# A two-layer graph network: transposes by DRAM scratch and VectorE block turns in place of TensorE, with TensorE in program order

## The chip, the core and the metric

The kernel runs on one core of a Trainium2 chip. TensorE (PE) multiplies, VectorE (DVE) and ScalarE (ACT) do elementwise work, GpSimd (POOL) one small power step, and SyncE (SP) issues the transfers. The metric is the device time of one execution in microseconds; lower is better.

## The reference

Thirty-two graphs (batches) of 512 nodes with 512 features go through two layers. All is float32.

```python
# layer 0
h = jnp.maximum(_layernorm(x, axis=-1), 0.0)
deg = jnp.sum(adj, axis=-1, keepdims=True)
agg = jnp.einsum('bij,bjf->bif', adj, h) / jnp.maximum(deg, EPS)
x = x + relu(einsum('bnf,of->bno', concatenate([h, agg], axis=2), W))
# layer 1
h = jnp.maximum(_layernorm(x, axis=-1), 0.0)
q, k = jnp.split(h @ Wqk, 2, axis=-1)
v = h @ Wv
agg = jnp.einsum('bij,bjd->bid', adj, k * mask[:, :, None])
w = inv_scale * mask * jnp.einsum('bid,bid->bi', q, agg)
x = x + softmax(w, axis=1)[:, :, None] * v
```

## The kernel before

**Algebra.** The weights are regrouped so that a batch needs six 512x512x512 products in five stages. Stage *y* is h times the second half of W (`layer0_y`, line 244). Stage *out* is h times the first half of W plus adj/deg times y (`layer0_out`, line 257; two products that accumulate together). Stage *u* is adj/deg times the masked h of layer 1 (`layer1_u`, line 299). Stage *t* is h of layer 1 times mR, where mR is Wq times Wk transposed, made once (`layer1_t`, line 310); its output is multiplied with u and summed along the rows, which gives w. Stage *v* is h of layer 1 times Wv (`layer1_v`, line 330).

**A product.** Each 512x512x512 product is cut in 2x2 blocks of 256 and computed with seven block products instead of eight (the Winograd form of Strassen's method; `product`, line 115). A tile of seven slots holds the four blocks of an operand and three sums of them; `left_sums` and `right_sums` compute the sums on DVE. Each block product is four matmuls of 128x128 by 128x256 per pair of operands (line 125). Three PSUM tiles pp, pr and pq take the results. Of these, partial results are copied to SBUF tiles called tmp by ScalarE (`keep`, line 138) before the next block product accumulates onto the same PSUM tile, so TensorE waits for such a copy if it is late. The final additions are on DVE.

**Transposes.** TensorE wants the left operand with its contraction dimension on the partitions, so h, adj/deg and h of layer 1 have to be transposed. `transpose_block` (line 160) does four 128x128 transposes on TensorE into a PSUM tile of the pool ps_t (two banks) and lets ScalarE write them to the left operand, with the ReLU on the way where it is needed. There are 12 such blocks a batch: four for h (pth, tile hT), four for adj (pta, tile aT), four for h of layer 1 (pt, tile h1T). The weights are transposed in the same way at the start (ptw).

**Order of the work.** One stream of stages runs on TensorE: for each i the loop at line 452 writes u of batch i-1, out of i, t and v of i-1, and y of i+1. After each block product, `step` (line 83) writes one piece of a list called `background`: statistics and normalization of the next batch (`prepare_h`, line 209), the degrees and transposes of adj (`prepare_a`, line 221), the normalization of layer 1 (`layer1_norm`, line 272, and `layer1_h`, line 285), and the softmax (`softmax`, line 344). What is left over is written out by `drain` at the end of a stage. This written order is a priority: a planner in the compiler orders each engine's queue by it, among the instructions that it takes to be ready, and sets the semaphores. Each engine then runs its own queue strictly in that planned order. A tile can be filled again only when the instructions that use its former content are done; how many copies a tile has ("bufs") limits how far ahead the loads run. SP issues all transfers from one queue.

The softmax needs three small matmuls on TensorE: ptop (line 363, turns the column of row maxima), pbc (line 368, spreads the maximum) and psum (line 375, sums the exponentials). Between them stand small steps on DVE and ACT. Four additions (line 380) then finish x, and one transfer stores it.

Of the kernel before, what the change touches and what calls it, by code (L numbers as in the profile page):

```python
# [21 lines left out]
def kernel(  # L22
# [26 lines left out]

    nc = tc.nc  # L50
    B, N, F = x.shape
    C = N // P
    D = F // P
    H = F // 2
    assert N == F == 512 and w0.shape[0] == F and wv.shape[1] == F
# [5 lines left out]
    ps_t = ctx.enter_context(tc.tile_pool(name="ps_t", bufs=2, space=bass.MemoryType.PSUM))  # L61
    ps_m = ctx.enter_context(tc.tile_pool(name="ps_m", bufs=5, space=bass.MemoryType.PSUM))
# [52 lines left out]
    def product(name, terms, out11, out12, out21, out22):  # L115
# [20 lines left out]
        def keep(p, what):  # L136
            t = block("tmp", 6, f"{what}_{name}")
            nc.scalar.activation(t, p, AF.Copy)  # L138
            return t
# [20 lines left out]
    def transpose_block(src, dst, func, name):  # L160

        p = ps_t.tile([P, 4, P], F32, tag="t", name=name)
        for d in range(4):
            nc.tensor.transpose(p[:, d, :], src[d], ident)  # L164
        nc.scalar.activation(dst, p.rearrange("p (a b) i -> p a b i", b=2), func)  # L165

    def row_blocks(t):
        return [t[:, ts(d, P)] for d in range(4)]

    def as_left(t, c):  # L170

        r = c // 2
        return t[:, 2 * r:2 * r + 2, :, ts(c % 2, P)]


    ident = const.tile([P, P], F32, name="ident")
    make_identity(nc, ident)
# [5 lines left out]
    X, HT, AT, DEG, Y, H1M, H1T, U, V, W = ({} for _ in range(10))  # L183

    def load_x(b):
        X[b] = big.tile([P, C, 512], F32, tag="x", bufs=3, name=f"x_{b}")
        nc.sync.dma_start(out=X[b], in_=x[b].rearrange("(c p) f -> p c f", p=P))

    def statistics(b, name):
        mv = small.tile([P, C, 2], F32, tag="mv", name=f"mv{name}")  # L190
        rstd = small.tile([P, C], F32, tag="rstd", name=f"rstd{name}")

        def one(c):
            st = small.tile([P, 6], F32, tag="st", bufs=4, name=f"st{name}_{c}")
            nc.vector.bn_stats(st, X[b][:, c, :])  # L195
            nc.vector.bn_aggr(mv[:, c, :], st)

        def last():
            nc.vector.tensor_scalar(rstd, mv[:, :, 1], LN_EPS, None, op0=ALU.add)  # L199
            nc.gpsimd.tensor_tensor(rstd, rstd, mhalf, op=ALU.pow)  # L200

        return mv, rstd, [lambda c=c: one(c) for c in range(C)] + [last]

    def normalize(o, i, mv, rstd, c):
        nc.vector.tensor_scalar(  # L205
            o, i, mv[:, c, 0:1], rstd[:, c:c + 1], op0=ALU.subtract, op1=ALU.mult
        )

    def prepare_h(b):

        mv, rstd, steps = statistics(b, f"0_{b}")
        HT[b] = slots("hT", 1, f"hT_{b}")

        def one(c):
            xn = chunk("xn", 2, f"xn_{b}_{c}")
            normalize(xn, X[b][:, c, :], mv, rstd, c)
            transpose_block(row_blocks(xn), as_left(HT[b], c), AF.Relu, f"pth_{b}_{c}")

        return steps, [lambda c=c: one(c) for c in range(C)] + left_sums(HT[b])

    def prepare_a(b):

        AT[b] = slots("aT", 2, f"aT_{b}")
        DEG[b] = small.tile([P, C], F32, tag="deg", bufs=3, name=f"deg_{b}")
        rdeg = small.tile([P, C], F32, tag="rdeg", name=f"rdeg_{b}")
        a = {}

        def one(c):
            a[c] = chunk("a", 3, f"a_{b}_{c}")
            nc.sync.dma_start(out=a[c], in_=adj[b, ts(c, P), :])  # L230
            nc.scalar.activation(a[c], a[c], AF.Copy, accum_out=DEG[b][:, c:c + 1])
            nc.vector.tensor_scalar(DEG[b][:, c:c + 1], DEG[b][:, c:c + 1], DEG_EPS, None, op0=ALU.max)
            nc.vector.reciprocal(rdeg[:, c:c + 1], DEG[b][:, c:c + 1])
            nc.scalar.activation(a[c], a[c], AF.Copy, scale=rdeg[:, c:c + 1])

        def two(c):
            transpose_block(row_blocks(a[c]), as_left(AT[b], c), AF.Copy, f"pta_{b}_{c}")

        steps = [lambda: one(0), lambda: one(1)]
        for c in range(C):  # L240
            steps.append(lambda c=c: (two(c), one(c + 2) if c + 2 < C else None))
        return steps + left_sums(AT[b])
# [14 lines left out]
    def layer0_out(b):  # L257
        def o(r, cc):
            dst = X[b][:, 2 * r:2 * r + 2, ts(cc, H)]

            def f(p, s):
                if s is not None:
                    t = block("tmp", 6, f"o_{b}_{r}{cc}")
                    add(t, p, s)
                    p = t
                nc.vector.scalar_tensor_tensor(dst, p, 0.0, dst, op0=ALU.max, op1=ALU.add)
# [5 lines left out]
    def layer1_norm(b):  # L272

        mv, rstd, steps = statistics(b, f"1_{b}")
        t = H1M[b] = slots("h1m", 1, f"h1m_{b}")

        def one(c):
            normalize(
                t[:, 2 * (c // 2):2 * (c // 2) + 2, c % 2, :],
                X[b][:, c, :].rearrange("p (a f) -> p a f", a=2), mv, rstd, c,  # L280
            )

        return steps + [lambda c=c: one(c) for c in range(C)]

    def layer1_h(b):

        t = H1M[b]
        l = H1T[b] = slots("h1T", 1, f"h1T_{b}")

        def one(c):  # L290
            k = c // 2
            src = [t[:, 2 * k + d // 2, c % 2, ts(d % 2, P)] for d in range(4)]
            transpose_block(src, as_left(l, c), AF.Relu, f"pt1_{b}_{c}")
            v = t[:, 2 * k:2 * k + 2, c % 2, :]
            nc.vector.tensor_scalar(v, v, 0.0, mraw[:, c, b:b + 1], op0=ALU.max, op1=ALU.mult)  # L295

        return [lambda c=c: one(c) for c in range(C)] + right_sums(t) + left_sums(l)

    def layer1_u(b):
        u = U[b] = big.tile([P, 4, 2, H], F32, tag="u", bufs=1, name=f"u_{b}")  # L300
# [9 lines left out]
    def layer1_t(b):  # L310
        acc = W[b] = small.tile([P, 2, C], F32, tag="acc", name=f"acc_{b}")

        def o(r, cc):
            def f(p, s):
                t = block("tmp", 6, f"t_{b}_{r}{cc}")
# [14 lines left out]
    def layer1_v(b):  # L330
        v = V[b] = big.tile([P, C, 512], F32, tag="v", bufs=1, name=f"v_{b}")
# [12 lines left out]
    def softmax(b):  # L344
# [16 lines left out]
        def s1():  # L361
            ptop = ps_s.tile([1, P], F32, tag="s", name=f"ptop_{b}")
            nc.tensor.transpose(ptop, top, ident)
# [15 lines left out]
        def s4(c):  # L379
# [4 lines left out]
            if c == C - 1:  # L384
                nc.sync.dma_start(out=out[b].rearrange("(c p) f -> p c f", p=P), in_=X.pop(b))
# [6 lines left out]
    def weight_rows(src, c, dst, name):  # L392
        t = chunk("a", 3, f"win_{name}_{c}")
        nc.sync.dma_start(out=t, in_=src[ts(c, P), :])
        transpose_block(row_blocks(t), dst, AF.Copy, f"ptw_{name}_{c}")

    def weight_right(src, dst, name):
        for c in range(4):
            weight_rows(src, c, dst[:, c // 2:4:2, :, ts(c % 2, P)], name)
# [3 lines left out]
    load_x(0)  # L403
    weight_right(w0[:, F:2 * F], w2R, "w2")
    steps, rest = prepare_h(0)
    for s in steps + rest:
        s()
    load_x(1)
# [3 lines left out]
    mask_sb = const.tile([B, N], F32, name="mask_sb")  # L412
    nc.sync.dma_start(out=mask_sb, in_=nodemask)
    wqT = big.tile([P, D, 512], F32, tag="u", bufs=1, name="wqT")
    wkT = big.tile([P, D, 512], F32, tag="v", bufs=1, name="wkT")
    for half, dst in ((0, wqT), (1, wkT)):
        for c in range(4):
            weight_rows(
                wqk[:, half * F:(half + 1) * F], c,
                dst[:, :, ts(c, P)].rearrange("p (a b) i -> p a b i", b=2), f"qk{half}",  # L420
            )
    for k in range(2):
        for dk in range(2):
            p = mm_tile(f"pm_{k}{dk}")
            d = 2 * k + dk
            for a in range(D):
                nc.tensor.matmul(
                    p.rearrange("p a f -> p (a f)"), wqT[:, a, ts(d, P)], wkT[:, a, :],
                    start=(a == 0), stop=(a == D - 1),
                )  # L430
            nc.scalar.activation(mR[:, 2 * k:2 * k + 2, dk, :], p, AF.Copy)
    for s in right_sums(mR):
        s()
    for k in range(2):
        for cc in range(2):
            nc.sync.dma_start(
                out=vR[:, 2 * k + cc, :, :],
                in_=wv[k * H:(k + 1) * H, ts(cc, H)].rearrange("(c p) f -> p c f", p=P),
            )
    for s in right_sums(vR):  # L440
        s()
    mcol = const.tile([P, C, B], F32, name="mcol")
    mraw = const.tile([P, C, B], F32, name="mraw")
    pmk = ps_t.tile([P, C, B], F32, tag="t", name="pmk")
    for c in range(C):
        nc.tensor.transpose(pmk[:, c, :], mask_sb[:, ts(c, P)], ident[:B, :B])
    nc.scalar.activation(mcol, pmk, AF.Copy, scale=scale)
    nc.scalar.activation(mraw, pmk, AF.Copy)
    drain()


    for i in range(B + 1):
        norm = prep = []
        if i > 0:
            layer1_u(i - 1)
            drain()
        if i + 1 < B:
            if i > 0:
                load_x(i + 1)
            steps, rest = prepare_h(i + 1)  # L460
            background += steps
        if i < B:
            layer0_out(i)
            drain()
            norm = layer1_norm(i)
# [44 lines left out]
```

## Time and profile before

| what | value |
|---|---|
| three runs | 2599.39, 2599.9 and 2601.4 us; median 2599.9 us |
| profiled execution | 2600.44 us, span 2598.7 us, mean granted TensorE clock 0.997 |
| TensorE busy | 2560.5 us, 99% of the span |
| VectorE, ScalarE, GpSimd busy | 1447.2, 814.0 and 65.2 us (56%, 31%, 3%) |
| HBM read, written | 72.42 MB, 33.55 MB |
| transposes on TensorE | 1,536 in the batches, 64 for the weights |

A line of a group reads: source line, engine, operation, output<-inputs, shape, count | busy time and mean duration in ns of one | idle time of the engine just before them, and what ended it. A line of a timeline reads: start, duration, engine, line, operation, output<-inputs, shape, count of merged instructions; in square brackets the idle time before it and what ended it. PE is matmuls, PEld is loading of the stationary operand. A matmul in float32 shows as two records. The busy times of successive matmuls overlap, so the spacing of their starts is the better price. A line of waits reads: who waited at which line <- for whom: total us, times, longest us. A line of a window reads: from:to, its length, then the busy time of PE, PEld, DVE, ACT and POOL, the granted clock, the mean busy share of the DMA engines and GB/s. A line of transfers reads: output<-input, issuing queue, operation, count, KB each, median us from issue to landing.

### The profile page before, as it was taken

The numbers are of one execution on the slowest core, as the hardware profiler recorded it, in microseconds if no ns is written. First come the engines' busy times: TensorE is split into PE (matmuls) and PEld (weight loads), VectorE is DVE, ScalarE is ACT, GpSimd is POOL, SyncE is SP. The second block draws the span as 40 slices with busy tenths as digits, with TensorE's granted clock in tenths as the row PEclk, the third lists the DMA queues.
The fourth block names the chain that finished last, engine by engine and source line by source line (L and its number), as shares of the span: only waits on it lengthen the run. The fifth ranks groups of instructions, "written<-read, shape, count | busy, mean of one in ns | idle before, by whom it ended". The sixth has DMA issues, their size and how long they took to land.

```text
span 2598.7 us, 31483 instructions
## 1 busy us (share of the span) xinstructions
PE 2560.5 (99%) x12548; PEld 2221.3 (85%) x12548; DVE 1447.2 (56%) x3410; ACT 814.0 (31%) x1559; POOL 65.2 (3%) x70
## 2 busy tenths in 40 slices
PE   7999999999999999999999999999999999999998
PEld 5888888888888888888888888888888888888887
DVE  4554555654655655556546556455565465565554
ACT  4333233332233332333322333323333223333222
POOL 0000000000000000000000000000000000000000
PEclk9999999999999999999999999999999999999999
DMA  4001011101111010111011110101110111101000
GB/s 159 17 17 50 33 49 49 42 24 44 38 49 49 17 49 33 49 49 46 21 45 37 49 49 17 49 33 49 49 36 30 44 38 49 49 17 49 33 21 33
DMA packets 55810, 107.98 MB, mean 42 GB/s; under 512 B 3408, under 2 KB 4432, under 8 KB 55664
## 3 DMA queue, kind: packets, MB, share of 16 engines
q1 hardware_dynamic: 55664, 105.99, 12.2%
q8 instruction: 98, 1.61, 0.3%
q14 instruction: 48, 0.39, 0.0%
HBM read 72.42 MB, written 33.55 MB: 41 GB/s over the span
## 4 chain that ended last, share of the span: by engine, by line
PE 91%; DMA 4%; ACT 2%; DVE 1%; issue 1%; POOL 0%; DVEq 0%; SPq 0%; ACTq 0%; POOLq 0%
PE pp_o L125 17%; PE pp_u L125 9%; PE pp_v L125 9%; PE pq_o L125 9%; PE pp_t L125 9%; PE pp_y L125 6%; PE pq_u L125 4%; PE pq_v L125 4%; PE pq_t L125 4%; PE pr_o L125 4%; PE pq_y L125 4%; DMA a<-in_adj_dram 3%; PE pr_v L125 2%; PE pr_t L125 2%; PE pth L164 2%; PE pt L164 2%
## 5 line engine op out<-in xcount | busy, mean ns | idle before, releaser
L195 DVE BATCH_NORM_STATS2 st<-x 128x6 f32<-128x512 f32 x256 | 165.7, 679 | 209.2 <-DMA x<-in_x_dram 207.1
L125 PE MATMUL pp_y<-w2R,hT 128*128 128x256 f32 x1024 | 253.1, 380 | 0.3 <-ACT hT L165 0.2
L125 PE MATMUL pp_u<-h1m,aT 128*128 128x256 f32 x1024 | 245.5, 382 | 0.0
L125 PE MATMUL pp_v<-vR,h1T 128*128 128x256 f32 x1024 | 242.1, 379 | 0.0
L125 PE MATMUL pp_t<-mR,h1T 128*128 128x256 f32 x1024 | 241.9, 379 | 0.0
L125 PE MATMUL pp_o<-w1R,hT 128*128 128x256 f32 x1024 | 241.9, 379 | 0.0
L125 PE MATMUL pp_o<-y,aT 128*128 128x256 f32 x1024 | 241.9, 379 | 0.0
L125 PEld LDWEIGHTS pp_o<-w1R,hT 128*128 128x128 f32 x1024 | 194.6, 190 | 26.9 <-issue 0.5
L125 PEld LDWEIGHTS pp_t<-mR,h1T 128*128 128x128 f32 x1024 | 194.6, 190 | 26.5
L125 PEld LDWEIGHTS pp_o<-y,aT 128*128 128x128 f32 x1024 | 194.6, 190 | 26.5
L125 PEld LDWEIGHTS pp_u<-h1m,aT 128*128 128x128 f32 x1024 | 189.6, 190 | 28.0 <-DVE h1m L295 0.3
L125 PEld LDWEIGHTS pp_v<-vR,h1T 128*128 128x128 f32 x1024 | 189.9, 190 | 23.3
L125 PEld LDWEIGHTS pp_y<-w2R,hT 128*128 128x128 f32 x1024 | 182.7, 191 | 19.4 <-ACT hT L165 0.5
L205 DVE TENSOR_SCALAR xn<-x,mv,rstd 128x512 f32<-128x512 f32 x128 | 67.1, 545 | 129.3 <-PE pth L164 91.4
L138 ACT ACTIVATE u_o<-pp_o 128x512 f32<-128x512 f32 x64 | 38.2, 597 | 295.2 <-PE pp_o L125 295.2
L92 DVE TENSOR_TENSOR o<-m_o,u_o 128x512 f32<-128x512 f32 x32 | 22.2, 692 | 194.1 <-ACT u_o L138 194.1
L200 POOL TENSOR_TENSOR rstd<-rstd,mhalf 128x4 f32<-128x4 f32 x64 | 64.5, 1008 | 2462.6 <-DVE rstd L199 2455.6
L125 PE MATMUL pq_u<-h1m,aT 128*128 128x256 f32 x512 | 123.6, 384 | 0.1
L125 PE MATMUL pq_y<-w2R,hT 128*128 128x256 f32 x512 | 121.7, 380 | 0.6 <-ACT m_y L138 0.4
L125 PE MATMUL pq_v<-vR,h1T 128*128 128x256 f32 x512 | 121.1, 379 | 0.0
L125 PE MATMUL pq_o<-y,aT 128*128 128x256 f32 x512 | 120.9, 379 | 0.0
L125 PE MATMUL pq_t<-mR,h1T 128*128 128x256 f32 x512 | 120.9, 379 | 0.0
(127 smaller groups left out, 4016.8 us busy)
## 6 DMA issues: line engine op xcount, KB each, us to landing
x<-in_x_dram SPq DMA_DIRECT2D x32, 1024.0 KB, 5.2
a<-in_adj_dram SPq DMA_DIRECT2D x128, 256.0 KB, 2.8
out_dram<-x SPq DMA_DIRECT2D x32, 1024.0 KB, 4.3
win_w<-in_L_gnn_W_dram SPq DMA_DIRECT2D x8, 256.0 KB, 4.7
win_qk<-in_L_gnn_Wqk_dram SPq DMA_DIRECT2D x8, 256.0 KB, 2.9
vR<-in_L_gnn_Wv_dram SPq DMA_DIRECT2D x4, 256.0 KB, 5.3
mask_sb<-in_nodemask_dram SPq DMA_DIRECT2D x1, 64.0 KB, 4.2
```

What stands on the lines that cost most here:

```text
L92: nc.vector.tensor_tensor(o, a, b, op=ALU.add)
L125: nc.tensor.matmul(p[:, rc, :], lt[:, LEFT[k], dk, ts(rc, P)], rt[:, RIGHT[k], dk, :], start=first and n == 0, stop=True, skip_group_check ...
L138: nc.scalar.activation(t, p, AF.Copy)
L164: nc.tensor.transpose(p[:, d, :], src[d], ident)
L195: nc.vector.bn_stats(st, X[b][:, c, :])
L200: nc.gpsimd.tensor_tensor(rstd, rstd, mhalf, op=ALU.pow)
L205: nc.vector.tensor_scalar(o, i, mv[:, c, 0:1], rstd[:, c:c + 1], op0=ALU.subtract, op1=ALU.mult)
```

## The change

The transposes leave TensorE. Instead:

1. The rows of a batch are laid on the partitions in another order: partition q*32+r holds, as chunk c, row q*128+c*32+r (`by_rows`). Each load or store of a batch becomes four transfers of 32 partitions.
2. The tensor to be transposed is written row by row to a scratch tensor in DRAM, chunk by chunk (`write` in `prepare_h`, `two` in `prepare_a`, `one` in `layer1_norm`).
3. `exchange` reads half of it back in four transfers, each of 32 partitions with pieces of 128 numbers (512 bytes), so that 32x32 blocks that belong on the same partitions lie there. `to_left` then turns the blocks with one VectorE instruction of 128x1024 into the left operand.
4. The normalization moves from VectorE to ScalarE (with the ReLU, `normalize`), which needs one more small VectorE step (`nmr`). In layer 1 ScalarE also scales by the mask, in place, after the unmasked rows were sent to DRAM.
5. x is loaded twice: once for the normalization (tag n), once for the residual (tag x, two buffers where there were three). u and v share one buffer, tmp has five buffers where it had six, and the matmul results have seven PSUM banks where they had five.
6. The loop is written under a manual schedule for TensorE: its instructions keep the written order, and only the other engines' are planned. The softmax steps are written ahead of the turns of layer 1's h, and the weights of layer 1 are made inside the first round of the loop (`weights_late`), after the first out.

The core of the diff:

```diff
-    ps_t = ctx.enter_context(tc.tile_pool(name="ps_t", bufs=2, space=bass.MemoryType.PSUM))
-    ps_m = ctx.enter_context(tc.tile_pool(name="ps_m", bufs=5, space=bass.MemoryType.PSUM))
+    dram = ctx.enter_context(tc.tile_pool(name="dram", bufs=2, space=bass.MemoryType.DRAM))
+    ps_m = ctx.enter_context(tc.tile_pool(name="ps_m", bufs=7, space=bass.MemoryType.PSUM))
...
-            t = block("tmp", 6, f"{what}_{name}")
+            t = block("tmp", 5, f"{what}_{name}")
...
-    def transpose_block(src, dst, func, name):
-        p = ps_t.tile([P, 4, P], F32, tag="t", name=name)
-        for d in range(4):
-            nc.tensor.transpose(p[:, d, :], src[d], ident)
-        nc.scalar.activation(dst, p.rearrange("p (a b) i -> p a b i", b=2), func)
+    def by_rows(src):
+        t = src.rearrange("(q c r) f -> q r c f", q=Q, c=C)
+        return [t[q] for q in range(Q)]
+
+    def exchange(src, name):
+        t = big.tile([P, 8, P], F32, tag="s", bufs=3, name=name)
+        for q in range(Q):
+            nc.sync.dma_start(out=t[q * R:(q + 1) * R, :, :], in_=src[:, :, ts(q, P)].rearrange("k r j -> r k j"))
+        return t
+
+    def to_left(src, h, dst, name):
+        t = exchange(src[h], name)
+        o = dst[:, 2 * h:2 * h + 2, :, :].rearrange("p a b (k r) -> p k (a b) r", r=R)
+        nc.vector.transpose(o, t.rearrange("p k (c r) -> p k c r", r=R))
...
+    def load_rows(tag, bufs, src, name):
+        t = big.tile([P, C, 512], F32, tag=tag, bufs=bufs, name=name)
+        for q, rows in enumerate(by_rows(src)):
+            nc.sync.dma_start(out=t[q * R:(q + 1) * R, :, :], in_=rows)
+        return t
...
-        nc.vector.tensor_scalar(
-            o, i, mv[:, c, 0:1], rstd[:, c:c + 1], op0=ALU.subtract, op1=ALU.mult
+        nc.scalar.activation(o, i, AF.Relu, scale=t[1][:, c:c + 1], bias=t[2][:, c:c + 1])
...
+        def write(c):
+            normalize(tiles[c], tiles[c], t, c)
+            nc.sync.dma_start(out=d[c], in_=tiles[c])
+
+        def turn(h):
+            if h == 0:
+                HT[b] = slots("hT", 1, f"hT_{b}")
+            to_left(halves(d), h, HT[b], f"sh_{b}_{h}")
...
         def one(c):
+            v = t[:, 2 * (c // 2):2 * (c // 2) + 2, c % 2, :]
+            normalize(v, X[b][:, c, :].rearrange("p (a f) -> p a f", a=2), mt, c)
+            nc.sync.dma_start(out=d[c].rearrange("p (a f) -> p a f", a=2), in_=v)
+            nc.scalar.activation(v, v, AF.Copy, scale=mraw[:, c, b:b + 1])
...
-        u = U[b] = big.tile([P, 4, 2, H], F32, tag="u", bufs=1, name=f"u_{b}")
+        u = U[b] = big.tile([P, 4, 2, H], F32, tag="uv", bufs=1, name=f"u_{b}")
...
-        v = V[b] = big.tile([P, C, 512], F32, tag="v", bufs=1, name=f"v_{b}")
+        v = V[b] = big.tile([P, C, 512], F32, tag="uv", bufs=1, name=f"v_{b}")
...
+    with tc.manual_schedule(engines={mybir.EngineType.PE}):
+        for i in range(B + 1):
...
+                layer0_out(i)
+                drain()
+                if i == 0:
+                    weights_late()
+                norm = layer1_norm(i)
...
-        background += (layer1_h(i) if i < B else []) + first + last
+            background += first + last + (layer1_h(i) if i < B else [])
+            if i + 1 < B:
+                layer0_y(i + 1)
             drain()
+            if i + 1 < B:
                 load_x(i + 1)
```

## The prediction

> **What bounds the kernel now.** I read the engine rows of the page first, then the granted clock and the chain that ended last, then TensorE's groups, and then one batch in order of time. The page:
>
> ```profile
> PE 2560.5 (99%) x12548; PEld 2221.3 (85%) x12548; DVE 1447.2 (56%) x3410; ACT 814.0 (31%) x1559; POOL 65.2 (3%) x70
> ...
> PEclk9999999999999999999999999999999999999999
> ...
> q1 hardware_dynamic: 55664, 105.99, 12.2%
> ...
> PE 91%; DMA 4%; ACT 2%; DVE 1%; issue 1%; POOL 0%; DVEq 0%; SPq 0%; ACTq 0%; POOLq 0%
> ...
> a<-in_adj_dram SPq DMA_DIRECT2D x128, 256.0 KB, 2.8
> ```
>
> TensorE is busy 99% at full clock and is 91% of the chain; the DMA engines are 12.2% used. So only less work on TensorE can help, and only if nothing new makes it wait. What goes is in TensorE's groups:
>
> ```profile
> L164 PE MATMUL pth<-ident,xn 128*128 128x128 f32 x512 | 77.7, 276 | 0.0
> L164 PE MATMUL pt<-ident,h1m 128*128 128x128 f32 x512 | 76.7, 273 | 1.0 <-ACT aT L165 1.0
> L164 PE MATMUL pta<-ident,a 128*128 128x128 f32 x512 | 75.3, 280 | 13.8 <-ACT a L234 13.8
> ```
>
> These busy times overlap their neighbours, so I price a transpose by what it shifts. TensorE's timeline, from 1269 us:
>
> ```profile
> 1269.63 1.89 PE L125 MATMUL pp_v<-vR,h1T 128*128 128x256 f32 x8
> 1271.36 0.60 PE L164 MATMUL pth<-ident,xn 128*128 128x128 f32 x4
> 1271.80 1.89 PE L125 MATMUL pq_v<-vR,h1T 128*128 128x256 f32 x8
> 1273.52 0.60 PE L164 MATMUL pth<-ident,xn 128*128 128x128 f32 x4
> ```
>
> A product of four matmuls (eight records) takes 1.73 us from start to start; a block of four transposes takes 0.44, or 0.434 averaged over several. The stages u, out, t, v and y of one batch, as windows:
>
> ```profile
> 1217.06:1229.92 12.86, 12.86 (x63) 11.08 (x61) 8.97 (x18) 3.29 (x6) 0.00 (x0) 1.00 0.21 79
> 1229.92:1254.09 24.17, 24.17 (x113) 21.28 (x112) 9.34 (x21) 2.99 (x5) 1.01 (x1) 1.00 0.14 46
> 1254.09:1266.18 12.09, 12.09 (x58) 10.64 (x56) 8.12 (x24) 2.39 (x4) 1.01 (x1) 1.00 0.00 1
> 1266.18:1280.02 13.84, 13.84 (x73) 12.15 (x72) 5.71 (x17) 4.45 (x8) 0.00 (x0) 1.00 0.00 0
> 1280.02:1296.38 16.36, 16.01 (x90) 13.69 (x89) 12.77 (x29) 11.87 (x25) 0.00 (x0) 1.00 0.22 65
> sum 79.32, PE 78.97 PEld 68.84 DVE 44.91 ACT 24.99 POOL 2.01; mean PE 15.79 PEld 13.77 DVE 8.98 ACT 5.00 POOL 0.40
> ```
>
> A batch takes 79.32 us: 42 products are 72.5, 12 transpose blocks 5.2, and 1.6 is left for softmax's small matmuls and gaps. Columns after the length are PE, PEld, DVE, ACT and POOL busy; DVE has 34 us free, ACT 54. The transposes are at most 6.6% of the period; that is all there is to win in the steady state.
>
> **The change part by part.** *TensorE.* From the start of the first u (106.04 us) to the end there are 240 blocks for h and adj (30 batches) and 124 for layer 1 (31): 364 x 0.434 = 158.0 us go. The waits of pta for ACT go too: 13.8 us less about 2.6 before 106 us = 11.2. Nothing covers them, since TensorE is the bound. [...]
>
> *VectorE.* Per batch 12 passes go (xn 0.524, h1m 0.499, mask 0.482 us for 128x512; 6.0 us) and six small degree steps of 0.16 (0.9). Six turns of 128x1024 come. No row shows one: the nearest full-rate passes bound it, twice the 0.482 of the mask step (0.97 us) and four times the 0.422 of the 128x256 multiply (1.69). I take twice the 0.687 of an add, 1.37: 8.2 us, and two scalar steps of 0.17. DVE goes from 45 to about 46.6 us of 74 and stays off the bound. [...]
>
> *ScalarE.* Twelve evictions of 0.593 us go (7.1), eight normalizations and four mask scalings come; at 0.60 to 0.72 (rows of L231 and L234) that is 7.2 to 8.6. ACT stays near 26 of 74 us.
>
> *DMA.* A batch moves 3 MB today. x comes twice, three tensors go to DRAM and come back: 10 MB. By bytes, 12.2% of 2598.7 us for 106 MB is 2.99 us per MB: 31 us. By packets at today's mean of 91 ns (12.2% x 16 x 2598.7 / 55664): 4,096 of 1 to 2 KB and 6,144 of 512 B on 16 engines are 58 us. Both fit under 74. SP issues 52 transfers a batch where it issued 6; at the 0.33 to 0.47 us of today's issues, 17 to 24 us. What is queued behind a waiting issue is the next load: x has only two buffers now, so its load waits for the store of the batch before last: y's end + 2 us for the last s4, + 4.3 landing, + 1.7 issuing, + 5.2 = about 13 us after y, against first use 12.1 + 3.45 x 2 + 0.7 = 19.7 us after it. Covered by u and the first two products of out; that cover gone, TensorE would wait through DVE's queue.
>
> *Distances.* The blocks for HT can turn as soon as out ends, and y needs them 24.2 us later; in t and v DVE has 13.8 of 25.9 us busy today. H1M, H1T and AT have 12 us or more each. u and v now share a buffer, with 3.45 us of products before v's first write. I cost these, the seven PSUM banks and the five tmp buffers at nothing (low end: the 0.8 us gap in y and the 0.8 in u also shrink, 1.6 x 31 = 49 us).
>
> *Program order on TensorE.* In the trace, softmax's small matmuls sit where they fit:
>
> ```profile
> 1296.27 0.27 PE L363 MATMUL ptop<-ident,top 128*1 128x128 f32 x1
> ...
> 1299.64 0.27 DVE L364 TENSOR_REDUCE ntop<-ptop 1x1 f32<-1x128 f32 x1
> 1299.97 0.29 PEld L368 LDWEIGHTS pbc<-ntop,ones 1*128 1x128 f32 x2 [0.37 <-DVE ntop L364]
> ...
> 1302.11 0.28 PE L375 MATMUL psum<-es,ones 128*128 128x1 f32 x2
> ```
>
> From ptop to pbc 3.7 us passed and to psum 2.1 more, because DVE had sums queued; two products ran meanwhile. In program order only one product (1.73) lies between each two. Bounds: 0, or (3.7 - 1.73) + (2.1 - 1.73) = 2.3 us a batch. The y sums that stood in front of ntop now come after it, so I take 1.0. Behind a waiting pbc stand all of y's remaining products.
>
> *A new wait on ScalarE.* The mask scaling overwrites h1m in place, so it waits until the transfer to DRAM has read it. Queued behind it are the keep copies, for which TensorE waits: it has 1.73 us less the 0.2 + 0.6 of the copy, some 0.93 of margin. The nearest row is ACT's wait for adj:
>
> ```profile
> ACT a L231 <- DMA a<-in_adj_dram: 27.9, 36, 1.3
> ```
>
> That is 0.87 us a batch for four such steps; lower end 0; upper end four whole landings past the margin, 4 x (2.8 - 0.93) = 7.5. I take 0.45, half the row, since the margin swallows part.
>
> *The start.* 106.04 us today up to the first u. By rows: x landed 7, statistics 10, moments 11.5, ScalarE 14, scratch write 17.5, read back and turn 23, sums 25.7; y from 21.5 to 34; out from 38 to 62; the weight product 16; y(1) 12; u at 91. Weights and scratch also share the queue (some 12 MB, 36 us by bytes, early). Bounds 90 and 120; I take 97: 9 saved.
>
> **Sum.** 2598.7 - 158.0 - 11.2 - 9.0 = 2420.5 span; new waits 1.45 x 31 = 45; span 2465. The profiled execution's own time is 2600.44, 1.7 above its span and 0.5 above the median of 2599.9: **2467 us**.
>
> **The rivals.** *No new wait*: DVE and ACT have room, and AT's, H1T's distances are long: 2420.5 + 1.7 = 2422. Against it: the 3.7 us above. *Slower, by ScalarE's wait for the scratch writes*: if all four landings come ahead of keep copies, 7.5 + 1.0 us a batch: 2422 + 264 = 2686. It decides from (2600 - 2422) / 31 = 5.75 us of new waits a batch. For it: the copies' margin is 0.93 and landings range from 2.5 to 5.0 us in the adj rows. Against: four such DMA-fed steps cost ACT 0.87 us today. *The transfers bound*: if a 512 B packet takes over (79.3 x 16 - 4096 x 0.091) / 6144 = 146 ns, the queue alone exceeds today's batch; at 182 ns it is 93 us, some 3050. No row shows a 512 B packet; against it, 91 ns is the mean with four times the bytes. *The transposes go but the order loses the gain*: 3 to 5.7 us of waits in y at ptop and pbc, 2515 to 2598.
>
> **How the numbers follow.** Likeliest, 0.5 to 3.5 us of waits: 0.50, own range 2435 to 2530. No new wait: 0.20. Order loses most: 0.06, and nothing left within 0.2%: 0.02. ScalarE's wait: 0.14, part of it just above 2600. Transfers: 0.08. So faster 0.76, same 0.02, slower 0.22 (0.2%, 5 us, is about what a measurement of this kernel can tell from no change). The range from 2400 (short start, gaps shrunk) to 2625 leaves out some 0.18.
>
> **What would show it.** Right: no L164 group, TensorE's records at 10,948 or so (12,548 less 1,536 and the 64 of the weights), a batch of 73.4 to 76 us, DVE near 46 us a batch, 10 MB a batch near 140 GB/s, the wait of pbc for ntop near 1 us. Wrong: rows where keep copies start late behind the mask scaling; y's first product waiting for HT's turn; a turn above 2 us; DMA share over 0.8; the granted clock below 1.00 where TensorE pauses; the first u after 120 us.

## The result, and the profile after

The changed kernel took 2954.55 us (2951.85 to 2955.24) against 2599.81 us for the kernel before on the same chip: 1.136 times as long, 95% interval 1.134 to 1.138. The forecast was 2467 us, with 0.76 for faster and a range of 2400 to 2625. It was wrong in sign and size. The profiled execution took 2955.12 us with a span of 2953.3 us.

The page of the kernel after, by the same lines as before, with the load of x's rows for the layer norm (tile n) added:

```profile
PE 2521.0 (85%) x10948; PEld 2145.5 (73%) x10948; DVE 1465.5 (50%) x3105; ACT 862.6 (29%) x1547; POOL 65.2 (2%) x70
...
PEclk8899999999999999999999999999999999999999
...
q1 hardware_dynamic: 363632, 340.96, 48.4%
...
PE 66%; DVE 12%; ACT 9%; DMA 6%; SPq 4%; issue 2%; POOL 1%; DVEq 0%; POOLq 0%; ACTq 0%
...
n<-in_x_dram SPq DMA_DIRECT2D x128, 256.0 KB, 6.8
```

TensorE issues the 10,948 matmuls that were forecast, 1,600 fewer than before. Yet its busy time fell by only 39.5 us (2560.5 to 2521.0), and its idle time rose from 38.2 to 432.3 us (span less busy). It is 66% of the chain now instead of 91%; VectorE, ScalarE, the transfers and SyncE's queue share the rest. The DMA engines are 48.4% used, so the transfers aren't the bound. What TensorE waits for, in total us, times, and the longest:

```profile
PE pp_y L131 <- DVE hT L183: 176.0, 31, 23.4
PE pq_v L131 <- ACT m_v L144: 132.3, 29, 4.9
PE pp_y L131 <- DVE hT L101: 68.0, 30, 2.3
...
PE pbc L414 <- DVE ntop L410: 0.7, 2, 0.4
```

The first three are 376 us of the 432. They come once a batch: stage y waits for the turned h of the next batch and then for its sums, and stage v waits for ScalarE's copies out of PSUM. One wait in the first line is another matter: the longest, 23.4 us, is that of the very first y at the start. The softmax wait, which the forecast priced at 1.0 us a batch, is 0.7 us in the whole run. The stages u, out, t, v and y of one batch, as windows (columns as in the table of the kernel before: length, then PE, PEld, DVE, ACT and POOL busy, granted clock, DMA share, GB/s):

```profile
1391.34:1404.04 12.70, 12.70 (x60) 11.18 (x59) 6.46 (x9) 2.98 (x5) 0.00 (x0) 1.00 0.94 227
1404.04:1428.21 24.17, 24.17 (x113) 21.28 (x112) 8.66 (x13) 2.98 (x5) 0.00 (x0) 1.00 0.52 104
1428.21:1440.30 12.09, 12.09 (x57) 10.64 (x56) 7.13 (x18) 2.39 (x4) 0.00 (x0) 1.00 0.00 0
1440.30:1465.40 25.10, 15.37 (x57) 12.42 (x56) 13.39 (x41) 11.04 (x17) 2.01 (x2) 0.81 0.63 157
1465.40:1483.40 18.00, 15.62 (x62) 12.60 (x62) 10.06 (x21) 7.32 (x17) 0.00 (x0) 0.88 0.24 74
sum 92.06, PE 79.95 PEld 68.12 DVE 45.70 ACT 26.71 POOL 2.01; mean PE 15.99 PEld 13.62 DVE 9.14 ACT 5.34 POOL 0.40
```

The stages u, out and t are what was forecast. Nearly all of the batch's loss is in the two rows with a clock below 1.00: v takes 25.10 us for the same number of products that t does in 12.09, and y takes 18.00. Of the batch, 12.1 us is idle (92.06 - 79.95). The busy time is also too long: after the pauses of 4.52 and 5.21 us in v and y the next product starts 3.57 and 3.55 us later instead of 1.73, and the granted clock of these two windows is 0.81 and 0.88. The timeline of the end of out, of v and of y shows one chain:

```profile
1422.14 0.69 DVE L98 TENSOR_TENSOR o<-m_o,u_o 128x512 f32<-128x512 f32 x1 [10.23 <-ACT u_o L144]
...
1441.84 1.29 DVE L210 BATCH_NORM_STATS2 st<-n 128x6 f32<-128x512 f32 x2
...
1447.24 2.93 ACT L221 ACTIVATE n<-n,nmr,rstd 128x512 f32<-128x512 f32 x4 [0.96 <-DVE nmr L217]
1450.16 2.92 ACT L221 ACTIVATE h1m<-x,nmr,rstd 128x512 f32<-128x512 f32 x4
1452.99 0.57 ACT L144 ACTIVATE m_v<-pq_v 128x512 f32<-128x512 f32 x1
1453.62 3.78 PE L131 MATMUL pq_v<-vR,h1T 128*128 128x256 f32 x8 [4.52 <-ACT m_v L144]
1457.19 3.00 PE L131 MATMUL pp_v<-vR,h1T 128*128 128x256 f32 x8
...
1462.08 2.02 DVE L101 TENSOR_TENSOR h1m<-h1m 128x512 f32<-128x512 f32 x3 [3.35 <-ACT h1m L327]
1464.02 2.36 DVE L183 STREAM_TRANSPOSE hT<-sh 128x1024 f32<-128x1024 f32 x2
1465.40 3.75 PE L131 MATMUL pp_y<-w2R,hT 128*128 128x256 f32 x8 [5.21 <-DVE hT L183]
```

The statistics of the next batch's rows (n) run at 1441.84, behind all of t's steps in VectorE's queue, although VectorE sat idle for 10.23 us ahead of 1422.14. So eight normalizations come to ScalarE in one piece, 5.85 us (2.93 + 2.92) in which the copy m_v waits behind them and TensorE waits for that copy. Then h must still be written, read back and turned: the turn is at 1464.02, 35.8 us after the end of out (1428.21), where y would have needed it after 24.2. The order in VectorE's queue costs something here too: the last read-back was issued by 1457.88 and none of these eight took over 4.4 us to land, so the turn's data were there by 1462.3, but the turn stood behind three sums of h1m, for which VectorE had idled 3.35 us. And the product that starts at 1453.62, after a pause of 4.52 us, is followed by the next after 3.57 us instead of 1.73.

### The profile page after: what moved, and what is told of

The parts are those of the page before. It is cut to its first block, busy times and chain, and to the rows that moved or that the text cites. A ratio compares the mean times of both kernels' runs of the same rounds, so it can differ in the third digit from the quotient of the medians.

```text
span 2953.3 us, 30565 instructions
## 1 busy us (share of the span) xinstructions
PE 2521.0 (85%) x10948; PEld 2145.5 (73%) x10948; DVE 1465.5 (50%) x3105; ACT 862.6 (29%) x1547; POOL 65.2 (2%) x70
## 2 busy tenths in 40 slices
DMA packets 363784, 342.91 MB, mean 116 GB/s; under 512 B 27216, under 2 KB 264784, under 8 KB 363632
## 3 DMA queue, kind: packets, MB, share of 16 engines
q1 hardware_dynamic: 363632, 340.96, 48.4%
## 4 chain that ended last, share of the span: by engine, by line
PE 66%; DVE 12%; ACT 9%; DMA 6%; SPq 4%; issue 2%; POOL 1%; DVEq 0%; POOLq 0%; ACTq 0%
PE pp_o L131 15%; PE pp_y L131 8%; PE pp_u L131 8%; PE pq_o L131 7%; PE pp_t L131 6%; PE pr_o L131 4%; PE pq_u L131 4%; SPq L176 4%; PE pq_t L131 4%; DVE st L210 4%; ACT h1m L221 3%; DMA n<-in_x_dram 3%; ACT a L276 3%; PE pq_y L131 2%; ACT n L221 2%
## 5 line engine op out<-in xcount | busy, mean ns | idle before, releaser
L131 PE MATMUL pp_y<-w2R,hT 128*128 128x256 f32 x1024 | 298.2, 442 | 244.2 <-DVE hT L183 176.0
L131 PEld LDWEIGHTS pp_y<-w2R,hT 128*128 128x128 f32 x1024 | 219.1, 222 | 300.9 <-issue 201.1
L131 PE MATMUL pq_v<-vR,h1T 128*128 128x256 f32 x512 | 171.9, 495 | 132.3 <-ACT m_v L144 132.3
L131 PE MATMUL pp_v<-vR,h1T 128*128 128x256 f32 x1024 | 257.4, 397 | 1.0 <-ACT m_v L144 1.0
L131 PEld LDWEIGHTS pq_v<-vR,h1T 128*128 128x128 f32 x512 | 126.3, 253 | 166.8 <-ACT m_v L144 144.0
L131 PEld LDWEIGHTS pp_v<-vR,h1T 128*128 128x128 f32 x1024 | 207.6, 203 | 35.1 <-ACT m_v L144 1.8
L131 PEld LDWEIGHTS pp_u<-h1m,aT 128*128 128x128 f32 x1024 | 195.2, 191 | 26.7
L131 PEld LDWEIGHTS pp_t<-mR,h1T 128*128 128x128 f32 x1024 | 194.6, 190 | 26.5
L131 PEld LDWEIGHTS pp_o<-w1R,hT 128*128 128x128 f32 x1024 | 194.6, 190 | 26.5
L131 PE MATMUL pq_y<-w2R,hT 128*128 128x256 f32 x512 | 128.1, 393 | 4.8 <-DVE hT L98 1.5
L101 DVE TENSOR_TENSOR h1m<-h1m 128x512 f32<-128x512 f32 x128 | 85.3, 687 | 90.2 <-ACT h1m L327 89.2
L144 ACT ACTIVATE u_o<-pp_o 128x512 f32<-128x512 f32 x64 | 38.2, 597 | 294.3 <-PE pp_o L131 294.3
```

Of the source, the lines that this page charges most:

```text
L101: nc.vector.tensor_tensor(o, a, b, op=ALU.subtract)
L131: nc.tensor.matmul(p[:, rc, :], lt[:, LEFT[k], dk, ts(rc, P)], rt[:, RIGHT[k], dk, :], start=first and n == 0, stop=True, skip_group_check ...
```

## The experiments

Two theories stood at first. *O*: the fixed order on TensorE makes the waits, since TensorE can't go on with another product. *Q*: SyncE's single queue of 52 transfers a batch is the cause, through the place of the loads in it. A third, *R*, is named in two expectations: the round trip through DRAM is too long by itself. The fourth, *V*, came up later, when a run missed: the planner's place for the statistics in VectorE's queue is the cause, wherever the rows are by then.

**TensorE's order given back to the planner** (no_order), and **the fixed order alone in the kernel before** (before_order). The edit to the kernel after, and the reverse to the kernel before:

```diff
-    with tc.manual_schedule(engines={mybir.EngineType.PE}):
+    if True:
         for i in range(B + 1):
```

> The changed kernel without the manual schedule: the planner orders TensorE too. If TensorE's fixed order is what costs (theory O), the waits of pq_v for ScalarE and of pp_y for the turned h shrink, because TensorE runs other matmuls meanwhile, and the time falls to 2450 to 2600 us. If the cause is that the rows of the next batch come late through SyncE's queue (theory Q), nothing that TensorE could run instead is ready in v and y, and the time stays within 2850 to 3050 us.

> The kernel before with only the manual schedule for TensorE in its loop. Theory O: over 2750 us, more than half of the loss of 355 us. Theory Q: the fixed order alone costs the softmax chain and a few waits of transposes for ScalarE, 1 to 3 us a batch: 2630 to 2700 us.

Without the fixed order the changed kernel took 2993.08 us (1.152, interval 1.150 to 1.154): 38 us more than with it. The wait of y for the turned h stays (233.0 us in total), and the softmax's psum waits 170.1 us. So O falls: the fixed order doesn't make the loss in this kernel, it saves a little of it. In the kernel before, though, the fixed order alone costs 390 us: 2989.71 us (1.151, 1.149 to 1.153), against the 2630 to 2700 of theory Q. That is the range O had named, over 2750, so this run by itself would have spoken for O; only no_order shows that the changed kernel loses its time elsewhere. Its TensorE timeline around the softmax:

```profile
1211.21 0.38 PE L368 MATMUL pbc<-ntop,ones 1*128 1x1 f32 x2 [3.42 <-DVE ntop L364]
...
1212.81 3.76 PE L125 MATMUL pp_u<-h1m,aT 128*128 128x256 f32 x8
```

There pbc waits up to 4.5 us a batch (107.6 us in all) and pta for adj 113.8 us. Besides, TensorE's busy time rises by 147 us (2560.5 to 2707.7) for the same 12,548 matmuls: the row of the product behind the wait is 3.76 us long instead of 1.89. The expectation had the waits in it, but not the clock, which is 0.943 on the mean here and 0.997 in the kernel before.

**Loads of n and adj issued by GpSimd** (n_pool), and **the written order on all five engines** (all_order):

```diff
-            n = load_rows("n", 2, x[b], f"n_{b}")
+            n = load_rows("n", 2, x[b], f"n_{b}", nc.gpsimd)
...
-            n = load_rows("n", 2, adj[b], f"a_{b}")
+            n = load_rows("n", 2, adj[b], f"a_{b}", nc.gpsimd)
```

> The changed kernel with the loads of n and adj issued from GpSimd's queue instead of SyncE's. Theory Q: the four parts of a load go out together, the statistics stand before t in VectorE's queue, the wait of pp_y for the turn falls from 176 us to under 40 and that of pq_v from 132 to under 40, the clock returns to 0.98 or more, and the time is 2430 to 2560 us. If the round trip through DRAM (normalize, write, read back, turn) is too long by itself for the 24 us of t and v (theory R), h is still late in y: 2800 to 2950 us.

> The changed kernel with all five engines' instructions in the written order, SyncE's issues too. Theory Q: the load of n is issued whole at the start of out, statistics and normalization follow in out, so h is turned by the end of v: waits of pp_y for hT under 60 us in total, 2480 to 2700 us. Theory R: y still waits 5 us or more a batch for h, 2800 us or more. Theory O gives no gain at all, since TensorE's order is the same: 2900 to 3000 us.

Eight issues of 52 moved to another queue made it 2470.06 us (0.951, 0.949 to 0.952). Page line, two of TensorE's waits, and the sum of the windows of one batch (t to out), of this kernel:

```profile
PE 2385.1 (97%) x10948; PEld 2065.0 (84%) x10948; DVE 1438.4 (58%) x3105; ACT 866.9 (35%) x1547; POOL 217.5 (9%) x326
```

```profile
PE pp_y L131 <- DVE hT L183: 35.9, 1, 35.9
...
PE pbc L414 <- DVE ntop L410: 2.8, 3, 1.4
```

```profile
sum 74.01, PE 73.63 PEld 64.27 DVE 44.12 ACT 26.91 POOL 6.81; mean PE 18.41 PEld 16.07 DVE 11.03 ACT 6.73 POOL 1.70
```

A batch takes 74.01 us, 18 less than after, and the wait of y for h comes once only, at the start. Against the kernel after the span is 485 us shorter: 349 less idle (432.3 to 83.2) and 136 less busy time (2521.0 to 2385.1) for the same 10,948 matmuls, with a mean granted clock of 0.994 instead of 0.941. Two things changed together here, however. In the kernel after the planner split the load of n: two parts go early and two wait behind other transfers, as SyncE's timeline shows:

```profile
1369.04 0.91 SPq L196 DMA_DIRECT2D n<-in_x_dram  x2
...
1404.73 0.90 SPq L196 DMA_DIRECT2D n<-in_x_dram  x2
```

The row of SyncE's longest wait in the kernel after shows what else its queue does:

```profile
SPq L243 <- ACT n L221: 1075.7, 128, 35.7
```

Line 243 writes the normalized n to scratch. SyncE issues nothing from 1407.86 to 1448.08, when that write goes out, and what is planned behind the write goes out after it: 33.6 us a batch on the mean, by which late statistics hold up the whole queue. With GpSimd issuing, the four parts go together at 1227.16, during y, and the planner puts the whole chain of n a batch earlier: the two turns of h start at 1271.71 and 1273.50, around the end of out (1272.22). So this run points to the load's queue, but it can't tell the late rows from the late place of the work on them. What GpSimd issues also goes by another DMA queue, in larger packets (q0, 20,480 packets for 67.13 MB; SyncE's q1 has 36,864 packets and 67.12 MB less than in the kernel after), which changes with the issuing engine.

The written order on all engines took 3491.94 us (1.344, 1.342 to 1.346). The wait for h did go (58.3 us), as Q had it; but the softmax's first step then stood behind the other work on VectorE (534.1 us of waits for `top`), so neither Q's nor O's time came. R's "2800 us or more" did, but without its sign: y waits for the turned h only twice in the run. For the four engines that the planner had ordered, the written order is the worse one here; which of them makes the difference, this run doesn't tell.

**One load at a time on GpSimd** (n_only, a_only), **the read-backs instead of the loads** (exch_pool), and **n_pool without the fixed order** (n_pool_no_order):

> The changed kernel with only the load of n on GpSimd's queue; adj stays on SyncE's. If it is n's own place in SyncE's queue that makes h late, this alone gives most of the gain: 2450 to 2600 us, waits of pp_y for the turn under 60 us. If it is the crowd on SyncE's queue as a whole, taking 4 of 52 issues away gives a tenth of the gain or less: 2850 us or more.

> The changed kernel with only the load of adj on GpSimd's queue; n stays on SyncE's. If n's own place decides, this gives little: 2850 us or more. If the crowd decides, it gives the same as moving n alone.

> The changed kernel with all loads on SyncE's queue and the reads back from scratch (24 issues a batch) on GpSimd's. If it matters that the load of n stands behind the reads back and their waits, this frees it as well: 2450 to 2600 us. If GpSimd's issues are slower (1 us or more each) or the load of n has to be on a queue of its own, 2750 us or more.

> n and adj on GpSimd's queue, and TensorE planned as in the kernel before. With the rows on time, the fixed order is either a help (then this is slower than 2470 us by 1 to 3 us a batch: 2500 to 2570) or without effect (2455 to 2490). If the fixed order cost something after all, it is below 2450 us.

n_only and a_only are the two halves of the edit above, n_pool_no_order is that edit with no_order's, and exch_pool replaces `nc.sync.dma_start` by `nc.gpsimd.dma_start` in `exchange`. The load of n alone gives 2597.04 us (0.999, 0.998 to 1.000), 357 us of the 484 between the medians; the load of adj alone 2863.71 us (1.101, 1.099 to 1.103), 91. With the loads left on SyncE and the 24 read-backs moved away it is 2478.96 us (0.954, 0.953 to 0.956). So it isn't the load's path as such: taking the read-backs out of SyncE's queue does nearly as much as taking the loads out. (There, too, the moved transfers go by q0 in larger packets, 184,432 packets on q0 and q1 together for 363,632; stats_first below leaves that out.) Without the fixed order n_pool is at 2457.82 us (0.946, 0.945 to 0.947), the fastest of all runs and better than both kernels; there the fixed order costs 12 us.

**The load of n written one stage earlier, all on SyncE** (n_early). The step `load` of batch i+2 is called ahead of the softmax of batch i-1, and not among the background work of the next pass:

```diff
-                steps, rest = prepare_h(i + 1)
-                background += steps
...
+                steps, rest = ahead
+                background += steps[1:]
...
+                if i + 2 < B:
+                    ahead = prepare_h(i + 2)
+                    ahead[0][0]()
                 first, last = softmax(i - 1)
```

> The changed kernel, all transfers on SyncE's queue, with the load of n for the next batch but one written right after v and so ahead of the softmax, the store, the reads back and the load of x. If n's place in the order is the cause (theory Q), the load goes out whole, the statistics stand before t in VectorE's queue and h is in time: 2480 to 2640 us, the wait of pp_y for hT below 80 us. If a queue of its own is what the loads need, the time stays above 2800 us.

It took 2799.95 us (1.078, 1.076 to 1.080): 155 us better than the kernel after, but far from the 2480 to 2640 that Q expected. The planner still split the load, and y still waited for the sums of h (118.5 us in all) and t for those of h1T (79.2). Writing the load earlier doesn't bring it out whole. This miss led to V.

**The statistics tied ahead in VectorE's queue, all transfers on SyncE** (stats_first). One ordering edge per batch puts out's second addition (that of m_o and u_o, block (1, 1)) behind the statistics of the next batch:

```diff
-        nc.vector.bn_aggr(t[0][:, c, :], st)
+        LAST[name[0]] = nc.vector.bn_aggr(t[0][:, c, :], st)
...
-                    add(t, p, s)
+                    z = add(t, p, s)
+                    if (r, cc) == (1, 1) and b + 1 < B:
+                        tc.add_manual_dep(z.ins, LAST["0"].ins.name, mybir.DependencyInfo(mybir.DependencyClass.NoSync, mybir.DependencyReason.DATA), reason="order")
```

> The changed kernel, all transfers on SyncE's queue, with one ordering edge a batch: VectorE's third eviction of out is placed behind the statistics of the next batch's rows, so the planned order on VectorE can't put them after t. If the rows had landed long before and only their place in VectorE's queue made h late (theory V), the statistics run some 25 us earlier, ScalarE normalizes in out, the wait of pq_v for ScalarE falls below 40 us and that of pp_y for the turn below 60: 2480 to 2620 us. If the split load itself is what is late (theory L), VectorE waits for it in out and the time stays above 2750 us.

It took 2597.39 us (1.000, 0.999 to 1.001): 357 us less than the kernel after, with every transfer still on SyncE's queue. VectorE's and ScalarE's timeline, where out starts at 1394.96:

```profile
1419.41 0.69 DVE L315 SCALAR_TENSOR_TENSOR x<-pp_o,x 128x512 f32<-128x512 f32 x1 [11.05 <-PE pp_o L131]
1420.01 1.28 DVE L212 BATCH_NORM_STATS2 st<-n 128x6 f32<-128x512 f32 x2
...
1424.89 2.93 ACT L223 ACTIVATE n<-n,nmr,rstd 128x512 f32<-128x512 f32 x4 [0.78 <-DVE nmr L219]
...
1441.52 1.24 DVE L183 STREAM_TRANSPOSE hT<-sh 128x1024 f32<-128x1024 f32 x1
...
1446.74 1.23 DVE L183 STREAM_TRANSPOSE hT<-sh 128x1024 f32<-128x1024 f32 x1
```

TensorE's wait of y for h in the same kernel, and then the window of t and the sum of the windows of the batch (out to u):

```profile
PE pp_y L131 <- DVE hT L183: 22.8, 1, 22.8
```

```profile
1419.13:1435.57 16.44, 12.88 (x57) 10.39 (x56) 12.20 (x36) 8.37 (x13) 2.01 (x2) 1.00 0.28 99
...
sum 78.10, PE 74.43 PEld 63.95 DVE 45.44 ACT 26.80 POOL 2.01; mean PE 14.89 PEld 12.79 DVE 9.09 ACT 5.36 POOL 0.40
```

The statistics run 25.05 us after the start of out; in the kernel after they ran at 37.8 us (1441.84 - 1404.04). So they come 12.8 us earlier and not the 25 expected, behind out's last eviction, for which VectorE idles 11.05 us, and ScalarE normalizes in t and not in out; the waits and the time came out as V had them. The load of n is split as before, two parts early and two at 1395.07. In the kernel after those two parts go out at 1404.73, and no transfer of n takes over 10.2 us to land, so they were there by 1416, 26 us ahead of their statistics. Not the rows were late, then, but the place of the work in VectorE's queue. One limit of this run: with the edge the planner placed other work of VectorE anew as well (the turns of h1T come 7.8 us after the start of out instead of 18.7), so it shows that the order decided, and the timeline argues that the statistics were the step. Theory R has something in it, though: from the statistics to the end of the second turn it takes 28.0 us here (1420.01 to 1447.97) and 24.5 in the kernel after (1441.84 to 1466.38), and t and v alone give 24.2. It fits here because t is longer, and in n_pool because the chain runs a batch earlier. The wait of y is left at the start alone, the wait of v for ScalarE's copies is no longer among the larger ones, and the mean clock is back from 0.941 to 0.990. What remains to n_pool, 127 us, lies in t: it takes 16.44 us instead of 12.09, and the batch 78.10 against 74.01, 31 times 4.09. TensorE waits for copies on ScalarE there (64.4 us for u_t, 42.6 for m_t), which now stand behind the normalizations that came forward.

**Two tries to better the best** (best_a: the first batch's loads back on SyncE; best_b: the load of x on GpSimd too):

> n and adj on GpSimd's queue from batch 1 on (batch 0 on SyncE's, whose first rows came at 8 us in the changed kernel and at 19 us with GpSimd's queue), and TensorE planned. The start gets 8 to 13 us shorter, the order is worth the 12 us seen: 2440 to 2452 us.

> As before, with the load of x on GpSimd's queue too. SyncE's wait for the store before the load of x (35 us in total) then holds nothing up: 2430 to 2452 us if that mattered, the same as without if not.

They took 2463.1 us (0.948, 0.947 to 0.950) and 2500.48 us (0.962, 0.961 to 0.964), both slower than n_pool_no_order. In best_a the first wait did fall from 34.7 to 23.0 us, but the start got longer all the same: the transpose of the mask (pmk) then waited 8.5 us instead of 0.4, and the first u came at 115.9 us instead of 112.2. The part behind it is another 2.1 us longer. In best_b TensorE waits for copies in v and t again (19.0 and 17.3 us). Each of these changes of a queue gave a new plan for the others too, and its effect wasn't foreseen either time.

## Why the prediction was wrong

- **The step that failed is "Distances".** The prediction said that the blocks for HT "can turn as soon as out ends, and y needs them 24.2 us later", and costed this at nothing. It priced the turn and looked for its buffer, but never followed the chain back from it: load, statistics, normalization, write, read back. That chain had the planner's order to pass on three engines. The statistics ran 13.6 us after the end of out and the turn 35.8 us after it, not at its end, and the term put at nothing cost y 176 + 68 us (23.4 of them at the start) and v 132 us of waits. Putting the statistics ahead in VectorE's queue (stats_first) gave 357 us back.
- **A second term was missing: the clock.** "The granted clock below 1.00 where TensorE pauses" was listed as a sign of being wrong, but had no price. In TensorE's busy time it is 136 us (mean granted clock 0.941 against 0.994), more than a quarter of the 485 us lost against n_pool. "y's first product waiting for HT's turn" was on that list too, and so was a first u after 120 us; all three signs appeared.
- **The gain was right, and was there to be had.** n_pool's edit changes only who issues two loads, and it took 2470 us against the forecast 2467. Its batch is 74.01 us, within the 73.4 to 76 named. From the first u to the end it takes 2350 us (2468.3 - 118.3) against 2492.7 before (2598.7 - 106.0): 142.7 saved, of the 169.2 that the transposes and pta's waits were worth. That leaves 26.5 us, 0.85 a batch, for new waits; 1.45 was taken. The start hid this: 97 us was forecast for the first u, it came at 124.0 after and 118.3 in n_pool. So that 2470 meets 2467 is partly luck: a start 21 us too long and waits 18 us too short nearly cancel.
- **VectorE, ScalarE.** The turn takes 1.235 us, inside 0.97 to 1.69 and below the 1.37 taken. Busy time per batch is 45.7 and 26.7 us for forecast 46.6 and 26. The turns weren't what made the changed kernel slow: with the same turns n_pool is 5% faster than the kernel before.
- **Transfers.** A packet takes 62.9 ns on the mean (48.4% x 16 x 2953.3 us / 363,632), against the 91 taken and the 146 of the rival; the rival of the transfers falls, though its 3050 us was nearest to the result. SyncE's 52 issues were mis-sized: in the batch shown the stretches in which they are issued add up to 30.6 us, not 17 to 24, since eight read-backs take 4.15 to 5.37 us, 0.52 to 0.67 from one to the next, though the median issue is 0.45. "Fits" was true of the total and missed what stands still in the queue: SyncE waits 1075.7 us in all for the normalized rows, with the rest of its transfers behind.
- **Program order on TensorE** was forecast at 1.0 us a batch for the softmax; pbc's wait is 0.7 us in all after and 2.8 in n_pool. The rival by which the order loses the gain falls for this kernel (no_order is slower still).
- **ScalarE's wait for the scratch writes**, the rival on the slower side, didn't come: the mask scaling waited 3.9 us in the whole run. It was near in one thing: copies out of PSUM did stand behind other ScalarE work. That work was the eight normalizations, 5.85 us in one piece, which no rival had.

What isn't settled: why the planner put the statistics behind t. That a shorter queue on SyncE brings the chain of n a batch forward (n_only, exch_pool) fits an estimate of readiness taken from that queue, but that is an argument, and no run shows the plan's own reasons. Nor does a run show by itself that ScalarE's order makes the remaining 127 us between stats_first and n_pool.

## What to carry to other kernels

When work moves off the bounding engine, follow each new chain back to its load, through the order of every queue that it passes, and price the distance between the last step and its use; enough room on an engine says nothing about the place in its queue. A wait on TensorE can cost twice, once as idle time and once as slow products behind it; here pauses of 3.42, 4.52 and 5.21 us did, and six of 27 pauses of 2.73. If a queue issues dozens of transfers a batch and a planner orders the other engines, try some of them on another queue, or an ordering edge, first: here that was worth 484 us, though the transfers weren't the bound.

## What the runs showed of the hardware

- **The products were slow after the longer pauses of TensorE, and after one length of pause, 2.73 us, some were slow and some not.** After pauses of 4.52 and 5.21 us in the kernel after, the next product started 3.57 and 3.55 us later instead of 1.73, in stages with a granted clock of 0.81 and 0.88; after one of 3.42 us before pbc and 0.77 more before psum in before_order, it was 3.55. After 1.67 us in stats_first it was 1.83. In between the same pause goes both ways, in n_only:

```profile
322.66 1.97 PE L131 MATMUL pp_t<-mR,h1T 128*128 128x256 f32 x8 [2.73 <-DVE h1T L101]
324.46 1.89 PE L131 MATMUL pq_t<-mR,h1T 128*128 128x256 f32 x8
...
638.52 3.65 PE L131 MATMUL pp_t<-mR,h1T 128*128 128x256 f32 x8 [2.73 <-DVE h1T L101]
642.01 1.89 PE L131 MATMUL pq_t<-mR,h1T 128*128 128x256 f32 x8
```

  Of the 27 pauses of 2.73 us in that run, 21 are followed by a start after 1.80 or 1.81 us and six by one after 3.19 to 3.54; the granted clock from 634 to 651 us is 0.90, and from 318 to 335 it is 1.00. Over a run, TensorE's busy time is 136 us longer in the kernel after than in n_pool and 147 us longer in before_order than in the kernel before, for the same numbers of matmuls.
- **Which engine issues a transfer mattered far beyond the time of the issue.** An issue of a part of n took 0.43 us on SyncE in the kernel after (median) and 0.55 on GpSimd in n_pool. The DMA engines were 48.4% used in the kernel after. Still, moving 8 of 52 issues gave 484 us, and a new plan of the other engines came with it. stats_first, which got 357 us back with every transfer on SyncE's queue, shows that most of this was the order of the work and not the transfers.
- **A block turn of 128x1024 in float32 on VectorE** takes 1.22 to 1.235 us on the mean for each of the three tensors (64 turns each, 75.9 to 79.0 us), 1.2 ns per column.
